# Half of the maximum's subtractions on VectorE in every block, and attention's context divided by its sums as it leaves PSUM

## The chip, the cores and the metric

The kernel runs on one core of one Trainium2 chip. A core has five engines that each work through a list of instructions of their own, in order: TensorE (PE, matrix products; its weight loads are listed apart as PEld), VectorE (DVE), ScalarE (ACT), GpSimd (POOL) and SyncE (SP), which here only issues DMA transfers. Engines wait for each other through semaphores. The metric is the time of one execution on the device in microseconds; the smaller, the better. The kernel before was run three times: 3268.8, 3256.43 and 3252.26 us, median 3256.43 us.

## The reference

One transformer layer in fp32: 2 sequences of 1024 tokens, width 1024, 32 heads of 32, and a gated feed-forward of 2752.

```
h   = layernorm(x)
qkv = h @ attn_qkvw + attn_qkvb                  # split into q, k, v, 32 heads of 32
scores = q @ k.T / sqrt(32)                      # per head, 1024 x 1024
probs  = softmax(scores)
x = x + (probs @ v) @ attn_ow + attn_ob
h = layernorm(x)
x = x + (silu(h @ W_gate.T) * (h @ W_up.T)) @ W_down.T
```

The softmax is the part that matters here: probs @ v = (exp(scores - max) @ v) / (sum of exp(scores - max)).

## The kernel before

**Blocks and units.** Tokens are worked on in four blocks of 512 (two sequences b, two halves blk). Attention of one block is 16 *units* (class Unit); a unit is two heads, 512 queries against 1024 keys, held as eight key tiles kt of 128 keys by 2 x 512 queries. A block then goes through the output projection and the feed-forward ("rest", lines 755 to 1148).

**A unit's way.** `scores` computes two key tiles at a time into PSUM; `largest` (L524, DVE) folds them into a running maximum `top`; `keep` (L529, ACT) copies them to SBUF as p. After the last tile `maximum` (L542 to L578) turns top, reduces it, and sends the negated maximum through DRAM to all partitions as `m`. Then, one key tile per beat, `less_maximum` (L580) adds m to p: L582 picks the engine, and `exponential` (L593, ACT) follows. `add` (L606) sums p over four neighbouring key tiles, on DVE for the last of each four (in the first block for all) and on POOL otherwise; the values are differenced to match (L599, POOL). `values` (L612) multiplies p by the values into the PSUM tile `acc`: columns 0 to 255 are the context, columns 256 to 511 the sums of p, by a matrix of ones, each sum repeated over the 32 rows of its head. There is one `acc` (bufs=1).

**From the accumulator to the projection.** `finish` (L638) copies acc to SBUF on ACT (L641) and later stores context and sums to DRAM (dctx L646, dsum L648). Every four units, `recip` (L703) loads the sums densely, takes reciprocals on DVE (L711) and stores them (drec). `load` (L719) brings a quarter of the context back with features on partitions (L722), loads each reciprocal row broadcast over 32 partitions (L726, eight loads a quarter), and POOL multiplies (L733). The event "prep" lets the output projection (`project` L782, products L785) start on that quarter.

**Order of the work.** Nothing is scheduled by hardware or compiler: the Emitter writes every engine's list in the order in which steps run here. Its clock counts only the planned cost of PE's steps (MM4 = 855 ns for a full product). `em.later(delay, fn)` issues fn when that clock has passed the delay. `run` takes side queues first (prep_ctx is one), then spreads the attention's beats (`paced`) evenly over the other work (`fill`). Attention of the first block runs beside the q, k and v projections; attention of blocks 2 to 4 runs beside the rest of blocks 1 to 3; the rest of block 4 runs alone. About 30 full products at the end of each rest (`late`, L1291) are held back and put ahead of the next projection.

**Feed-forward.** Gate and up are seven products of quarter matrices for each chunk of 128 features (Strassen-Winograd; `product`, L927), each ending in a PSUM tile that ACT (L939) or DVE (L941 to L954) reads out; silu is on ACT (L955), h = gate * up on DVE (L957). Every four chunks the down product follows in the same manner (`down7`, L1076): its PSUM tiles are added into x by DVE, one or two instructions each (L1089, L1091), and DVE forms four sums over h (L1045 to L1051). The last two chunks of a block use plain products (L1003, read out at L1014), and DVE puts x's halves right (L1032, L1034). All these products, the projections and the transposes (L259) share three PSUM tiles (`lps`, bufs=3).

Of the kernel before, what the change touches and what calls it, by code (L numbers as in the profile page):

```python
# [12 lines left out]
ALU = mybir.AluOpType  # L13
AX = mybir.AxisListType

P = 128
HEADS = 32
HD = 32
NH = 512
# [111 lines left out]
def preln_block_kernel(  # L131
# [14 lines left out]
    nc = tc.nc  # L146
# [64 lines left out]
    def dtile(shape, name):  # L211
        return dram.tile(shape, F32, tag=name, name=name)
# [4 lines left out]
    dv = {(b, hf): dtile([S, NH], f"dv{b}_{hf}") for b in range(B) for hf in range(NHF)}  # L217
    blocks = [(b, blk, i) for b in range(B) for blk in range(NS) for i in range(QTR)]
    dctx = {k: dtile([H // QTR, NH], "dctx%d_%d_%d" % k) for k in blocks}
    dsum = {k: dtile([HEADS // QTR, NH], "dsum%d_%d_%d" % k) for k in blocks}  # L220
    drec = {k: dtile([HEADS // QTR, NH], "drec%d_%d_%d" % k) for k in blocks}


    dws = [dtile([P, 4, NH], f"dws{c}") for c in range(NFULL)]
# [240 lines left out]
    class Unit:  # L465
# [113 lines left out]

        def less_maximum(self, kt):  # L580
            p = self.p[kt]
            eng = nc.vector if self.phase == 0 and kt % 4 == 3 else nc.gpsimd  # L582
            eng.tensor_tensor(p, p, self.m, ALU.add)  # L583
            em.later(3500.0, lambda: self.exponential(kt))
            if kt % SUMS > 0:

                vec = self.phase == 0 or kt % RUN == RUN - 1
                delay = 8100.0 if self.phase == 0 else 10000.0 if vec else 9500.0
                eng = nc.vector if vec else nc.gpsimd
                em.later(delay, lambda: self.add(kt, eng))  # L590
# [47 lines left out]
        def finish(self):  # L638
            part, n = divmod(self.u, UNITS // QTR)
            cs = Sm(f"cs_{self.name}")  # L640
            nc.scalar.copy(cs, self.acc)  # L641
            key = self.b, self.blk, part

            def store():
                ctx_ = dctx[key][n * 2 * HD : (n + 1) * 2 * HD, :]
                nc.sync.dma_start(ctx_.rearrange("f (a q) -> a f q", a=2), cs[:, :NQ])  # L646
                sums = dsum[key][2 * n : 2 * n + 2, :].rearrange("h (a q) -> a h q", a=2)
                nc.sync.dma_start(sums, cs[::HD, NQ:])  # L648

            em.later(2500.0, store, ("ctx", self.n))  # L650

# [48 lines left out]
    def prep_ctx(b):  # L700


        def recip(blk, i):  # L703
            cols = HEADS // QTR * NH // P
            sm = small([P, cols], "sums", 1, f"sums_{b}_{blk}_{i}")
            flat = lambda d: d.rearrange("h s -> (h s)").rearrange("(p c) -> p c", p=P)
            nc.sync.dma_start(sm, flat(dsum[b, blk, i]))
            rc = small([P, cols], "recs", 1, f"recs_{b}_{blk}_{i}")

            def go():  # L710
                nc.vector.reciprocal(rc, sm)  # L711
                nc.sync.dma_start(flat(drec[b, blk, i]), rc)

            em.later(11000.0, go, ("rec", b, blk, i))

        def alloc(blk):
            ctxT[b, blk] = T(f"ctx_{b}_{blk}")

        def load(blk, i):  # L719
            n = KC // QTR  # L720
            part = ctxT[b, blk][:, i * n : (i + 1) * n, :]
            nc.sync.dma_start(part, dctx[b, blk, i].rearrange("(g p) n -> p g n", p=P))  # L722
            recs = [Sm(f"rec_{b}_{blk}_{i}_{g}") for g in range(n)]
            for g, rec in enumerate(recs):
                for j in range(HPG):
                    nc.sync.dma_start(  # L726
                        rec[j * HD : (j + 1) * HD, :],
                        drec[b, blk, i][g * HPG + j, :].partition_broadcast(HD),
                    )

            def go():
                for g, rec in enumerate(recs):
                    nc.gpsimd.tensor_tensor(part[:, g, :], part[:, g, :], rec, ALU.mult)  # L733

            em.later(5000.0, go, ("mult", b, blk, i))
            em.later(8000.0, lambda: None, ("prep", b, blk, i))

        per = UNITS // QTR
        recips, loads = Steps(), Steps()
        for blk in range(NS):  # L740
            for i in range(QTR):
                n = (b * NS + blk) * UNITS + (i + 1) * per - 1
                recips.add(lambda blk=blk, i=i: recip(blk, i), needs=("ctx", n))
            if blk > 0:
                free = ("gu", b, blk - 1)
            else:
                free = ("half", B - 1) if b == 0 else ("gu", b - 1, NS - 1)
            loads.add(lambda blk=blk: alloc(blk), needs=free)
            for i in range(QTR):
                if i > 0:  # L750
                    loads.add(lambda: None, needs=("mult", b, blk, i - 1))
                loads.add(lambda blk=blk, i=i: load(blk, i), needs=("rec", b, blk, i))
        return recips, loads

    def oproj_steps(q, b, blk, st):
        st["w"] = {}
# [456 lines left out]
    with tc.manual_schedule():  # L1213

        head, fill, keep_qk = Steps(), Steps(), Steps()

        def two(fn, *args, **kw):

            q = Steps()
            fn(q, *args, **kw)  # L1220
            return q

        def ln_steps(q, b, t0, t1, tools, ahead):

            load, norm, turn, _ = tools
            for t in range(t0, t1):
                if t + ahead < t1:
                    q.add(lambda t=t + ahead: norm(t))
                turn(q, t)
                if t + 5 < NT:  # L1230
                    q.add(lambda t=t + 5: load(t))

        tools = load, norm, turn, _ = ln1(0)
        for t in range(4):
            head.add(lambda t=t: load(t))
        head.add(lambda: nc.sync.dma_start(bqk_t, b_qk))
        for _ in range(4):
            head.add(wst.next)
        head.add(lambda: load(4))
        for _ in range(8):  # L1240
            head.add(dst.next)
        for _ in range(5):
            head.add(wst.next)
        head.add(lambda: norm(0))
        ln_steps(head, 0, 0, TB, tools, 1)
        for _ in range(2):
            head.add(dst.next)
        qk_steps(head, 0, 0, [0])
        head.add(lambda: norm(TB))
        side = two(ln_steps, 0, TB, NT, tools, 1)  # L1250
        head.items += merged(two(v_steps, 0, 0, range(TB)), side).items
        qk_steps(head, 0, 0, [1])

        v_steps(fill, 0, 0, range(TB, NT))
        for g in range(1, G // 2):
            qk_steps(fill, 0, g)
        v_steps(fill, 0, 1)
        for g in range(G // 2, G - 2):
            qk_steps(fill, 0, g)

        tools = load1, norm1, turn1, stats1 = ln1(1)
        for t in range(5):
            fill.add(lambda t=t: load1(t))
        qk_steps(fill, 0, G - 2, [0])
        fill.items += merged(two(qk_steps, 0, G - 1, [0]), stats1(0, TB)).items
        last = two(qk_steps, 0, G - 2, [1])
        qk_steps(last, 0, G - 1, [1])
        fill.items += merged(last, two(ln_steps, 1, 0, TB, tools, 1)).items
        fill.items += merged(two(v_steps, 1, 0, range(2)), stats1(TB, TB)).items
        fill.items += merged(  # L1270
            two(v_steps, 1, 0, range(2, TB)), two(ln_steps, 1, TB, NT, tools, 1)
        ).items
        v_steps(fill, 1, 0, range(TB, NT))
        for g in range(0, G // 2):
            qk_steps(fill, 1, g)
        v_steps(fill, 1, 1)
        for g in range(G // 2, G - 2):
            qk_steps(fill, 1, g)
        for s in range(NS):
            for g in range(G - 2, G):  # L1280
                qk_steps(keep_qk, 1, g, [s])
            if s == 0:
                keep_qk.add(lambda: None, gives=("half", 1))

        def rest(n):

            q, late, st = Steps(), Steps(), {}
            b, blk = divmod(n, NS)
            turn = oproj_steps(q, b, blk, st)
            ffn_steps(q, b, blk, st, turn)  # L1290
            while late.cost < 30 * MM4:  # L1291
                late.items.insert(0, q.items.pop())
            return q, late


        rests = [rest(n) for n in range(B * NS)]
        lists = attention_steps([(n + 1) * UNITS * NT + 2 * NT for n in range(B * NS - 1)])
        side = [*prep_ctx(0), *prep_ctx(1)]
        em.run(head)
        em.run(fill, lists[0], side=(*side, weight_sum_steps()))  # L1300
        keep = keep_qk
        for (q, late), beats in zip(rests, [*lists[1:], None]):
            em.run(joined([keep, q]), beats, side=side)
            keep = late
        em.run(keep)
        em.settle(True)
# [51 lines left out]
```

## Time and profile before

| | |
|---|---|
| runs of the kernel, us | 3268.8, 3256.43, 3252.26 (median 3256.43) |
| profiled execution: span from first to last instruction, us | 3272.8 |
| its time beyond the span | not shown on the page; the span stands for the execution |
| mean granted TensorE clock | 0.986 |
| PE busy | 3166.3 us, 15488 products |
| DVE busy | 2012.2 us, 2733 instructions |
| ACT busy | 1446.8 us, 1585 instructions |
| POOL busy | 2039.6 us, 1079 instructions |
| subtraction of the maximum on POOL (L583) | 480 of 2508 ns |
| the same on DVE (first block only) | 32 of 1882 ns |
| copy of the accumulator on ACT (L641) | 64 of 588 ns |
| multiplication by the reciprocals on POOL (L733) | 32 of 1338 ns |
| DMA | 507.24 MB, mean 155 GB/s |

How to read it: the profile is one execution. A group's line gives source line, engine, operation, output<-input with shapes, count, then busy time and mean duration, then the idle time of the engine just before these instructions and what ended most of it. The 40 slices each stand for 3272.8 / 40 = 81.8 us; a digit is a busy share in tenths, and PEclk is the clock granted to TensorE in tenths of full speed. Stages by the timeline: first block's attention from 180 to 880 us, then boundary and rest of block 1 (880 to 1480), of block 2 (1480 to 2140), of block 3 (2140 to 2760), and of block 4 to the end. "Body" below means the stretches 1000 to 1480, 1640 to 2140 and 2310 to 2760 us.

### The profile page before, as it was taken

To read this page: it belongs to the slowest core of one execution; us is meant where nothing else is said; L and a number is where in the kernel's file an instruction comes from. 1 tells how busy PE (TensorE), PEld (TensorE's weight loads), DVE (VectorE), ACT (ScalarE), POOL (GpSimd) and SP (SyncE) were. 2 spreads that over 40 slices of the span, in tenths; PEclk is the share of its full clock that TensorE was granted. 3 is DMA by queue.
4 is the path that set the end of the run, shared out by engine and by line. 5 is a ranking of instruction groups with operands and counts; after the bars stand their busy time and mean duration, and the time that the engine had idled before them with its cause. 6 is when DMAs were issued, how large, how long until landed. Compare 5 with 4: busy or idle time off the path is not lost.

```text
span 3272.8 us, 42759 instructions
## 1 busy us (share of the span) xinstructions
PE 3166.3 (97%) x15488; PEld 1785.6 (55%) x15488; DVE 2012.2 (61%) x2733; ACT 1446.8 (44%) x1585; POOL 2039.6 (62%) x1079
## 2 busy tenths in 40 slices
PE   8999999999999999998899999988999999999999
PEld 4444434444346666563376655633756567477775
DVE  2266766776356777766577777666777774344334
ACT  2244554544456555563665555635655554010000
POOL 0267766777788777667887777777877777200000
PEclk9999999999999999998999999989999999999999
DMA  4566756655434554555344444562445445544452
GB/s 154 167 182 203 228 181 197 195 186 164 145 109 139 155 150 150 149 153 180 98 146 150 148 146 146 151 184 92 140 146 151 149 140 149 168 152 154 153 153 96
DMA packets 337825, 507.24 MB, mean 155 GB/s; under 512 B 105424, under 2 KB 122064, under 8 KB 337616
## 3 DMA queue, kind: packets, MB, share of 16 engines
q1 hardware_dynamic: 281424, 405.91, 40.4%
q10 hardware_dynamic: 56192, 98.60, 9.8%
q8 instruction: 124, 2.03, 0.3%
q14 instruction: 85, 0.70, 0.1%
HBM read 429.14 MB, written 75.24 MB: 154 GB/s over the span
## 4 chain that ended last, share of the span: by engine, by line
PE 79%; DVE 8%; POOL 4%; DMA 3%; issue 3%; ACT 2%; SPq 1%; ACTq 0%; POOLq 0%; DVEq 0%
PE p L927 30%; PE pq L371 13%; PE pd L1076 9%; PE acc L622 8%; PE s L510 7%; PE pvv L433 6%; PE po L785 4%; POOL p L583 2%; DVE x L1089 2%; DVE top L524 1%; DVE p L606 1%; PE pd L1003 1%; PE pg L971 1%; POOL p L606 1%; DVE h L957 1%
## 5 line engine op out<-in xcount | busy, mean ns | idle before, releaser
L583 POOL TENSOR_TENSOR p<-p,m 128x1024 f32<-128x1024 f32 x480 | 1197.0, 2508 | 15.9 <-DMA m<-d 15.9
L529 ACT COPY p<-s 128x1024 f32<-128x1024 f32 x512 | 516.3, 1012 | 730.0 <-DVE top L524 553.6
L593 ACT ACTIVATE p<-p 128x1024 f32<-128x1024 f32 x512 | 529.6, 1056 | 379.2 <-POOL p L583 325.6
L606 POOL TENSOR_TENSOR p<-p,p 128x1024 f32<-128x1024 f32 x192 | 466.8, 2431 | 352.5 <-ACT p L593 346.8
L524 DVE TENSOR_TENSOR top<-s,top 128x1024 f32<-128x1024 f32 x384 | 469.1, 1222 | 289.0 <-PE s L510 272.0
L927 PE MATMUL p<-sum,m 128*128 128x256 f32 x2688 | 610.4, 382 | 1.4 <-ACT gate L939 0.9
L927 PEld LDWEIGHTS p<-sum,m 128*128 128x128 f32 x2688 | 505.2, 190 | 101.1 <-issue 29.3
L927 PE MATMUL p<-xn2T,m 128*128 128x256 f32 x2016 | 469.5, 384 | 0.3 <-ACT xn2T L267 0.2
L371 PE MATMUL pq<-xnT,wqk 128*128 128x512 f32 x1024 | 457.4, 599 | 0.0
L1076 PE MATMUL pd<-wp,h 128*128 128x512 f32 x960 | 432.6, 598 | 15.2 <-DVE x L1089 15.0
L927 PEld LDWEIGHTS p<-xn2T,m 128*128 128x128 f32 x2016 | 382.6, 192 | 87.0 <-issue 29.8
L606 DVE TENSOR_TENSOR p<-p,p 128x1024 f32<-128x1024 f32 x192 | 328.1, 1709 | 105.2 <-ACT p L593 70.4
L371 PEld LDWEIGHTS pq<-xnT,wqk 128*128 128x128 f32 x1024 | 190.2, 190 | 249.4 <-issue 247.7
L510 PE MATMUL s<-q,k 32*128 32x512 f32 x2048 | 312.6, 650 | 12.0 <-ACT p L529 12.0
L1076 PEld LDWEIGHTS pd<-wp,h 128*128 128x128 f32 x960 | 177.7, 190 | 251.1 <-issue 197.0
L1189 POOL TENSOR_TENSOR ws<-raw 128x512 f32<-128x512 f32 x62 | 89.8, 1448 | 298.3 <-DMA raw<-in_w_gu 190.7
L1089 DVE TENSOR_TENSOR x<-pd,x 128x512 f32<-128x512 f32 x360 | 235.7, 680 | 52.6 <-PE pd L1076 52.2
L622 PE MATMUL acc<-p,vals 128*32 128x256 f32 x4096 | 254.6, 389 | 11.3 <-DVE p L606 11.3
L433 PE MATMUL pvv<-wv,xnT 128*128 128x512 f32 x512 | 231.1, 601 | 0.2 <-DVE vv L445 0.2
L785 PE MATMUL po<-wo,ctx 128*128 128x512 f32 x512 | 229.7, 601 | 0.8 <-DMA wo<-in_w_o 0.8
L622 PEld LDWEIGHTS acc<-p,vals 128*32 128x32 f32 x4096 | 121.4, 111 | 181.6 <-issue 97.7
L990 POOL MEMSET h<- 64x512 f32 x4 | 2.1, 524 | 298.9 <-PE pd L1076 298.9
(94 smaller groups left out, 2520.2 us busy)
## 6 DMA issues: line engine op xcount, KB each, us to landing
m<-dws SPq DMA_DIRECT2D x336, 256.0 KB
m<-in_w_gu SPq DMA_DIRECT2D x252, 256.0 KB
wp<-ddn SPq DMA_DIRECT2D x160, 256.0 KB
m<-d SPq DMA_DIRECT2D x64, 512.0 KB
wp<-in_w_dn SPq DMA_DIRECT2D x120, 256.0 KB
raw<-in_w_gu ACTq DMA_DIRECT2D x84, 256.0 KB
dws<-ws ACTq DMA_DIRECT2D x84, 256.0 KB
x<-in_x SPq DMA_DIRECT2D x32, 512.0 KB
```

Source lines behind the costliest of these rows:

```text
L371: nc.tensor.matmul(ps, wqk[b, g, w, hk][:, k, :], xnT[b, s][:, kc, :], start=(kc == 0), stop=(kc == KC - 1),)
L433: nc.tensor.matmul(st["ps"], xnT[b, t // TB][:, kc, (t % TB) * P : (t % TB + 1) * P], st["w"][kc], start=(kc == 0), stop=(kc == KC - 1),)
L510: nc.tensor.matmul(ps[a][:, h * NH : (h + 1) * NH], self.k[rows, i * P : (i + 1) * P], self.q[rows, :], start=True, stop=True,)
L524: nc.vector.tensor_tensor(self.top, s, self.p[0] if kt == 1 else self.top, ALU.max)
L529: nc.scalar.copy(self.p[kt], s)
L583: eng.tensor_tensor(p, p, self.m, ALU.add)
L593: nc.scalar.activation(self.p[kt], self.p[kt], AF.Exp, scale=SCALE)
L606: eng.tensor_tensor(self.p[kt], self.p[kt], self.p[kt - 1], ALU.add)
L622: nc.tensor.matmul(self.acc[j * HD : (j + 1) * HD, c : c + NQ], w(h), self.p[kt][:, q0 : q0 + NQ], start=start, stop=stop, skip_group_chec ...
L785: nc.tensor.matmul(st["ps"], ctxT[b, blk][:, g, t * P : (t + 1) * P], st["w"][hf, g], start=(g == 0), stop=(g == G - 1),)
L927: nc.tensor.matmul(ps, mats[c, n][:, kc, :], rhs, start=(kc == 0), stop=(kc == hk - 1),)
L1076: nc.tensor.matmul(st["pd"], lefts[n](pi)[:, j, t * P : (t + 1) * P], st["wp", pi, n, j], start=(j == 0), stop=(j == PART // 2 - 1),)
```

## The change

Two things change. In `less_maximum`, DVE took key tiles 3 and 7 in the first block and none after it; now it also takes the odd key tiles (1, 3, 5, 7) of the units of blocks 2 to 4. In `finish`, the context is divided by its sums as it leaves PSUM: DVE takes the reciprocal of the 256 columns of sums and multiplies the 256 columns of context by it. The copy on ACT, the sums' way through DRAM, the broadcast loads, and POOL's multiplication fall away. The quarter's context is loaded as soon as its store has been issued; no quarter waits for the multiplication of the one before; "prep" comes 6000 ns of planned time after the load instead of 8000.

```diff
         def less_maximum(self, kt):
             p = self.p[kt]
-            eng = nc.vector if self.phase == 0 and kt % 4 == 3 else nc.gpsimd
+            mine = kt % 4 == 3 if self.phase == 0 else kt % 2 == 1
+            eng = nc.vector if mine else nc.gpsimd
             eng.tensor_tensor(p, p, self.m, ALU.add)
...
             cs = Sm(f"cs_{self.name}")
-            nc.scalar.copy(cs, self.acc)
+            nc.vector.reciprocal(cs[:, NQ:], self.acc[:, NQ:])
+            nc.vector.tensor_tensor(cs[:, :NQ], self.acc[:, :NQ], cs[:, NQ:], ALU.mult)
...
                 nc.sync.dma_start(ctx_.rearrange("f (a q) -> a f q", a=2), cs[:, :NQ])
-                sums = dsum[key][2 * n : 2 * n + 2, :].rearrange("h (a q) -> a h q", a=2)
-                nc.sync.dma_start(sums, cs[::HD, NQ:])
...
-        def recip(blk, i):
...
-            def go():
-                nc.vector.reciprocal(rc, sm)
-                nc.sync.dma_start(flat(drec[b, blk, i]), rc)
-
-            em.later(11000.0, go, ("rec", b, blk, i))
...
             nc.sync.dma_start(part, dctx[b, blk, i].rearrange("(g p) n -> p g n", p=P))
-            recs = [Sm(f"rec_{b}_{blk}_{i}_{g}") for g in range(n)]
...
-            def go():
-                for g, rec in enumerate(recs):
-                    nc.gpsimd.tensor_tensor(part[:, g, :], part[:, g, :], rec, ALU.mult)
-
-            em.later(5000.0, go, ("mult", b, blk, i))
-            em.later(8000.0, lambda: None, ("prep", b, blk, i))
+            em.later(6000.0, lambda: None, ("prep", b, blk, i))
...
-                if i > 0:
-                    loads.add(lambda: None, needs=("mult", b, blk, i - 1))
-                loads.add(lambda blk=blk, i=i: load(blk, i), needs=("rec", b, blk, i))
-        return recips, loads
+                n = (b * NS + blk) * UNITS + (i + 1) * per - 1
+                loads.add(lambda blk=blk, i=i: load(blk, i), needs=("ctx", n))
+        return loads
```

More of the change, by code (lines that the diff above doesn't have):

```diff
@@ L219, in preln_block_kernel @@
     dctx = {k: dtile([H // QTR, NH], "dctx%d_%d_%d" % k) for k in blocks}
-    dsum = {k: dtile([HEADS // QTR, NH], "dsum%d_%d_%d" % k) for k in blocks}
-    drec = {k: dtile([HEADS // QTR, NH], "drec%d_%d_%d" % k) for k in blocks}
     dws = [dtile([P, 4, NH], f"dws{c}") for c in range(NFULL)]
@@ L700, in prep_ctx @@
     def prep_ctx(b):
-        def recip(blk, i):
[L704 to L708, printed above, removed]
-            def go():
-                nc.vector.reciprocal(rc, sm)
-                nc.sync.dma_start(flat(drec[b, blk, i]), rc)
-            em.later(11000.0, go, ("rec", b, blk, i))
         def alloc(blk):
@@ L722, in load @@
             nc.sync.dma_start(part, dctx[b, blk, i].rearrange("(g p) n -> p g n", p=P))
-            recs = [Sm(f"rec_{b}_{blk}_{i}_{g}") for g in range(n)]
-            for g, rec in enumerate(recs):
[L725 to L729, printed above, removed]
-            def go():
-                for g, rec in enumerate(recs):
-                    nc.gpsimd.tensor_tensor(part[:, g, :], part[:, g, :], rec, ALU.mult)
-            em.later(5000.0, go, ("mult", b, blk, i))
-            em.later(8000.0, lambda: None, ("prep", b, blk, i))
+            em.later(6000.0, lambda: None, ("prep", b, blk, i))
         per = UNITS // QTR
-        recips, loads = Steps(), Steps()
+        loads = Steps()
         for blk in range(NS):
-            for i in range(QTR):
-                n = (b * NS + blk) * UNITS + (i + 1) * per - 1
-                recips.add(lambda blk=blk, i=i: recip(blk, i), needs=("ctx", n))
             if blk > 0:
@@ L1297, in preln_block_kernel @@
         lists = attention_steps([(n + 1) * UNITS * NT + 2 * NT for n in range(B * NS - 1)])
-        side = [*prep_ctx(0), *prep_ctx(1)]
+        side = [prep_ctx(0), prep_ctx(1)]
         em.run(head)
```

## The prediction

> **What bounds the kernel now.** I read the page from the top: busy shares, the 40 slices, the chain that ended last. Then the waits of the whole span, the stages with a low PE digit, and the stretches in which the kernel multiplies by the down weights.
>
> ```profile
> span 3272.8 us, 42759 instructions
> ...
> PE 3166.3 (97%) x15488; PEld 1785.6 (55%) x15488; DVE 2012.2 (61%) x2733; ACT 1446.8 (44%) x1585; POOL 2039.6 (62%) x1079
> ...
> PE   8999999999999999998899999988999999999999
> ...
> PEclk9999999999999999998999999989999999999999
> ...
> PE 79%; DVE 8%; POOL 4%; DMA 3%; issue 3%; ACT 2%; SPq 1%; ACTq 0%; POOLq 0%; DVEq 0%
> ```
>
> TensorE (PE) is the bound: 97% busy, 79% of the chain. The change touches no matmul, so it can only move the 3272.8 - 3166.3 = 106.5 us in which PE is idle, and the granted clock behind those gaps. DVE at 61% and POOL at 62% look free, but that is a mean over stages. Both low digits of PE and of the clock lie where one 512-token block ends and the next begins. The view by windows, cut at the stages, says how low (columns: window, PE, PEld, DVE, ACT, POOL, clock, DMA share, GB/s):
>
> ```profile
> 1480.00:1640.00 160.00, 135.43 (x631) 59.20 (x628) 96.60 (x124) 74.37 (x80) 127.66 (x70) 0.91 0.43 134
> 1640.00:2140.00 500.00, 491.90 (x2840) 311.71 (x2839) 362.48 (x516) 282.63 (x301) 389.68 (x195) 1.00 0.50 149
> 2140.00:2310.00 170.00, 141.49 (x662) 64.86 (x661) 103.33 (x123) 79.66 (x87) 128.21 (x70) 0.90 0.41 128
> ```
>
> At the boundaries POOL is at 75 to 80%, PE idles 25 and 29 us, and the clock is 0.91 and 0.90, which costs about 0.09 x 160 = 14 and 0.10 x 170 = 17 us more. The timeline of the second boundary shows why (start, duration, engine, line; in brackets the idle time before and its releaser):
>
> ```profile
> 2164.30 1.26 POOL L733 TENSOR_TENSOR ctx<-ctx,rec 128x512 f32<-128x512 f32 x1 [5.52 <-DMA rec<-drec]
> ...
> 2175.72 3.35 DVE L606 TENSOR_TENSOR p<-p,p 128x1024 f32<-128x1024 f32 x1 [11.50 <-POOL p L606]
> ...
> 2179.73 2.07 PE L1003 MATMUL pd<-wd,h 128*128 128x512 f32 x2 [11.70 <-DVE x L1014]
> ```
>
> POOL stands at L733 for the broadcast reciprocals, its subtractions behind that are late, DVE stands in L606 for POOL's sum, DVE's evacuation (L1014) is queued behind, and PE waits 11.70 us for it. The same row costs 8.48 us at 1516.
>
> **What goes.** (1) The detour of the sums: 64 stores, 16 loads and 16 stores of them, 128 broadcast loads on SP's queue, 16 reciprocals (5.5 us of DVE), 32 multiplications on POOL (42.5 us) with 97.2 us of waiting for DMA. What stops PE through it, by PE's gaps in the timeline: 3.2 + 8.5 at 1500 to 1516, 1.7 + 11.7 at 2156 to 2168, and 8.4 at 2243 where POOL, still late, ran ops back to back and one DVE addition took 12.18 us: 33.5 us. The trace's records of the granted clock have half-clock stretches at these gaps (6.8, 10.2, 13.7, 3.4, 10.2 us) cost half of 44.3 = 22 us. At 885 to 900, where POOL also waits for rec, 3.2 us of gaps and half a 6.8 us window are 6.6 us. That is 62 us at most. What is late next there are DVE's own evacuations in the last down stretch and the last token tile's layernorm (pt_f waits for ACT gate L939, 15.3 us in all, untouched). I take 45 us, and 20 as the lower bound. Before the new loads, prep needs 6 us of planned time instead of 8, and PE holds over 25 us of held-back matmuls (30 x 0.855) to cover them; uncovered, each of the 4 blocks could lose one landing, a few us.
>
> (2) POOL gives up 4 of 8 subtractions in 48 units: 192 x 2.5 = 480 us, off the path in the body, where PE is 98 to 99% busy. It is worth something at the boundaries alone, within the 45.
>
> (3) ACT's 64 copies cs<-acc at 0.588 us: 38 us off ACT (44% busy), worth nothing by themselves.
>
> **What comes, all on DVE.** (a) 192 subtractions. The row for them is L583 DVE in the first block: x32, mean 1882 ns beside a POOL busy 72%; at best they take what L606 takes when POOL is quiet, 1216 ns. In the body POOL falls to about half busy, so I take 1.7. (b) 64 times a reciprocal of 128x256 and a product of 128x256 from PSUM. The product has a row, L949: 424 ns. The reciprocal has 128x32 at 342 ns and 128x4 at 178: (342 - 178) / 28 = 5.9 ns a column, so 178 + 252 x 5.9 = 1.65 us; bounds are 0.42 (any other 128x256) and 8 x 0.342 = 2.74. Together 2.07 us.
>
> The Trainium skill (VectorE: DVE Perf Modes, on the fixed hardware budget) says that reciprocal repeats its divide 8 times; at the 0.96 GHz of its page Trainium Kernel Development and Optimization (NeuronCore Architecture), 256 columns would be an estimated 2.13 us instead of 1.65, some 31 us more over 64 units. The skill also speaks against (a): by its page SBUF — State Buffer (two separate sides), a DVE op with two SBUF inputs and a POOL op exclude each other for the whole instruction, so the moved work would still wait for POOL. The rows agree as far as they go: h (L957) takes 0.69 us at the end without POOL and 1.24 to 1.69 beside it.
>
> Is there room? A unit (two heads) takes some 39.7 us in the body, DVE is busy 72% there, about 28.4 us. 4 x 1.7 + 2.07 = 8.9 us more, less some 0.7 us of shorter waits for POOL, makes 36.6, 92%. That fits on average, but not where it counts. The stretches of down products (L1076) have two DVE evacuations for many PSUM tiles and four sums over h. The windows view of the 14 such stretches that run beside attention (the last rows and their sum):
>
> ```profile
> 2376.80:2409.50 32.70, 31.09 (x122) 12.27 (x121) 31.60 (x40) 13.80 (x16) 22.91 (x10) 1.00 0.42 130
> 2475.80:2506.60 30.80, 30.71 (x122) 12.46 (x121) 29.89 (x40) 15.61 (x17) 23.00 (x13) 1.00 0.53 157
> 2572.80:2604.90 32.10, 31.03 (x122) 12.44 (x121) 30.95 (x40) 14.20 (x16) 22.54 (x9) 1.00 0.44 135
> 2672.30:2703.30 31.00, 30.64 (x122) 12.55 (x121) 29.17 (x41) 15.81 (x16) 25.97 (x14) 1.00 0.44 137
> sum 458.80, PE 440.70 PEld 179.70 DVE 418.09 ACT 205.88 POOL 321.18; mean PE 31.48 PEld 12.84 DVE 29.86 ACT 14.71 POOL 22.94
> ```
>
> DVE is busy 418.1 of 458.8 us, 91%; 40.7 us are free, and PE already loses 18.1 us waiting for evacuations. 96 maxima (L524) start in these stretches, 96 / 7 = 13.7 units. They bring 55 subtractions (67 us at 1.22, 104 at 1.89) and 13.7 x 2.07 = 28 us. POOL goes from 70% to (321 - 55 x 2.36) / 459 = 42%; of about 45 us by which the sums over h exceed their 0.68 us, some 18 go. Net 77 to 114 us, middle 95. Of the 40.7 free us a third to all can be used, since DVE runs in order and some idle time lies before the products end; and DVE may come out of each stretch 1 us later than now (the three PSUM buffers are already used up: lags of 4 to 6 us). So PE loses 95 - 41 - 14 = 40 to 95 - 12 - 14 = 69 us more, and I take 55; with the ends of both prices 22 to 88. In the product stretches (L927) DVE is busy 4 to 8 us of 10 and most of 2 to 5 us more fits: 8 us, 0 to 15.
>
> Queued behind each reciprocal, which waits for the accumulator, are the subtraction and the next evacuations; scores and both maxima are issued ahead of it and outlast the accumulator's 2.5 us, so the wait is about nothing. The store of cs comes 1.5 us later or more and holds SP's queue, with weights loaded several tiles ahead as cover. In the first block only 2.07 us a unit are added, on a DVE busy 459 of 700 us: 0, up to 5. DVE's first subtraction follows POOL's by one beat; POOL waited only 15.9 us for m in all, but DVE is less late than POOL: 0 to 10, I take 0.
>
> **Sum.** -45 + 55 + 8 + 0 = +18 us against the profiled execution: 3272.8 becomes 3291. The page gives only its span, no time around it, and that is 16 us above the median; as a difference on the median: 3256.4 + 18 = 3274.
>
> **Rivals.**
> - *Down stretches hold DVE's load (faster).* It decides if the subtractions cost about 1.22 us (POOL half idle, few waits) and all free time is used: loss 77 - 41 - 14 = 22, gain 55 to 62. Net about -36: 3220. For it: POOL's own lateness makes many of DVE's waits. Against: 91% busy already, and PE idle there. It turns below 45 us of loss. 0.30.
> - *DVE bound through the whole body.* Each subtraction waits for a POOL op, or for m at the boundaries, and the product stretches cannot drain the lag: loss 88 + 15 + 5, gain 30: +78, 3334. For it: 92% and about 0.9 us of unavoidable waiting for silu per chunk. 0.17.
> - *Nothing arrives.* The stalls at the boundaries are re-made by the next late engine and DVE's work finds room: 3256. 0.08.
> - Forecast, slower by a little: 0.45, its own range 3258 to 3300.
>
> About 0.5% (16 us) is what a measurement of this kernel can tell from no change. Of the forecast's 0.45, 0.27 lies over that and 0.18 within; of the first rival 0.28 is faster, 0.02 within. Faster 0.28, same 0.28, slower 0.44. The range takes in the first two rivals' middles: 3222 to 3335.
>
> **What would show it.** Right: L733 and L711 gone, no gap over 5 us at the boundaries and clock above 0.95 there; L583 DVE at 1.5 to 1.9 us x224; a reciprocal of about 1.65 us; DVE over 95% and PE's idle time 60 to 90 us in the 14 stretches. Wrong: PE idle below 45 us there (first rival), or PE below 97% between the stretches too (second). A reciprocal far from 1.65 us, or a boundary that still idles 25 us, would each refute a term.

## The result and the profile after

The changed kernel takes 3312.77 us (median of 4 runs, 3310.75 to 3314.07) against 3256.74 us before (4 runs): ratio 1.0154, 95% interval 1.0131 to 1.0178, 56 us slower. The sign was forecast; the size was not (18 us). From the page of the changed kernel, the lines that answer to those shown of before:

```profile
span 3310.0 us, 42267 instructions
...
PE 3173.4 (96%) x15488; PEld 1775.4 (54%) x15488; DVE 2339.7 (71%) x3037; ACT 1416.2 (43%) x1521; POOL 1601.0 (48%) x855
...
PE   8999989999999999998899999988999999999999
...
PEclk9999999999999999999999999999999999999999
...
PE 73%; DVE 21%; ACT 3%; issue 2%; DMA 1%; ACTq 0%; SPq 0%; DVEq 0%
```

PE still sets the end, but DVE's part of the chain went from 8 to 21%. The digits of the clock no longer dip. The same two boundaries in the view by windows, here cut from the end of a block's last full down stretch to the next block's first gate product (window, PE, PEld, DVE, ACT, POOL, clock, DMA share, GB/s), first before, then after:

```profile
1497.70:1618.90 121.20, 105.21 (x464) 43.20 (x464) 70.03 (x88) 60.46 (x64) 105.42 (x56) 0.93 0.42 133
2153.80:2284.30 130.50, 107.20 (x466) 43.41 (x465) 77.31 (x87) 59.10 (x63) 103.06 (x56) 0.90 0.39 121
```

```profile
1513.80:1620.60 106.80, 101.20 (x466) 41.43 (x464) 85.14 (x99) 51.87 (x54) 71.15 (x36) 0.97 0.39 125
2186.90:2295.40 108.50, 101.55 (x465) 41.62 (x463) 87.51 (x104) 51.82 (x54) 71.33 (x36) 0.97 0.39 124
```

The boundaries are 14 and 22 us shorter with the same products, PE's idle time there falls from 16 and 23 to 6 and 7 us, and POOL's busy time from 105 and 103 to 71 us. So what was meant to be won was won. The loss is inside the blocks. The 15 stretches of gate and up products of blocks 1 to 3, last line of the same view for before, then after:

```profile
sum 1080.90, PE 1064.24 PEld 781.62 DVE 673.76 ACT 651.03 POOL 859.62; mean PE 70.95 PEld 52.11 DVE 44.92 ACT 43.40 POOL 57.31
```

```profile
sum 1124.80, PE 1073.33 PEld 776.11 DVE 855.73 ACT 641.72 POOL 632.30; mean PE 71.56 PEld 51.74 DVE 57.05 ACT 42.78 POOL 42.15
```

And the 14 down stretches, after (before: 458.8 us, PE 440.7, DVE 418.1, shown with the prediction):

```profile
sum 503.10, PE 453.96 PEld 178.84 DVE 479.25 ACT 209.21 POOL 229.54; mean PE 32.43 PEld 12.77 DVE 34.23 ACT 14.94 POOL 16.40
```

Product stretches +44 us, down stretches +44 us, everything else 1733 to 1682 us, -51: together the 37 us by which the profiled spans differ. Of the first 44 us, 35 are idle time of PE (17 us before, 51 after) and 9 are longer busy time; of the second, 31 (18 before, 49 after) and 13. Part of the 13 is the clock: it is 1.00 in all 14 down stretches before, and 0.91 to 0.96 in four of them after, which by their rows is worth some 8.5 us (an estimate). The second stretch, before and after:

```profile
1164.70:1196.90 32.20, 30.49 (x122) 12.52 (x121) 30.35 (x39) 14.52 (x16) 22.57 (x10) 1.00 0.46 138
1165.80:1204.10 38.30, 33.28 (x122) 13.19 (x121) 35.62 (x46) 14.21 (x15) 16.11 (x8) 0.91 0.35 108
```

In the down stretches DVE is 95% busy; in the product stretches it is 76% busy on average and PE idles 51 us all the same. PE waits for the reading-out (evacuation) of its PSUM tiles. In the view of waits (us in total, times, longest us), first the down products, before and after, then two of the gate and up products after, where before has nothing over 0.9 us (L1044, L1057 and L895 are before's L1076, L1089 and L927):

```profile
PE pd L1076 <- DVE x L1089: 17.9, 26, 1.7
PE pd L1044 <- DVE x L1057: 47.5, 43, 5.0
...
PE p L895 <- DVE gate L918: 6.8, 6, 2.3
PE p L895 <- DVE gate L911: 4.9, 5, 1.7
```

What that looks like in a product stretch: the timeline of DVE in the changed kernel, at the end of a unit.

```profile
1865.17 2.56 DVE L522 TENSOR_TENSOR top<-s,top 128x1024 f32<-128x1024 f32 x2 [0.57 <-PE s L508]
1867.64 1.75 DVE L640 RECIPROCAL cs<-acc 128x256 f32<-128x256 f32 x1
1869.42 0.42 DVE L641 TENSOR_TENSOR cs<-acc,cs 128x256 f32<-128x256 f32 x1
1869.76 3.03 DVE L582 TENSOR_TENSOR p<-p,m 128x1024 f32<-128x1024 f32 x1
1872.71 0.41 DVE L911 TENSOR_TENSOR gate<-p,gate 128x256 f32<-128x256 f32 x1
```

Two maxima, the reciprocal, the product and the subtraction of key tile 3 stand in one beat, 7.6 us in which no feed-forward tile is read out (L911 is the first again). PE meanwhile works 2.3 us on the accumulator and fills its three PSUM tiles (24 matmuls), then waits:

```profile
1867.36 5.45 PE L895 MATMUL p<-sum,m 128*128 128x256 f32 x24
1873.18 1.13 PE L895 MATMUL p<-sum,m 128*128 128x256 f32 x4 [0.37 <-DVE gate L911]
```

In this unit the beat just fits, and PE waits 0.37 us; in the unit at 1656, with the same five instructions, it waits 1.53 us. Counted over the trace, 31 such beats lie in product stretches, and 17 us of PE's idle time there stand directly behind them (within ten DVE instructions from the reciprocal on). Another 12 us stand further on, while DVE is still late or waits; 22 us (15 before) stand ahead of the transposes behind layernorm.

The subtraction is 3.03 us long in the unit shown. By key tile, the mean over 48 units is 1.40 us for tile 1, 2.26 for 3, 1.23 for 5 and 1.94 for 7: 45 of the 48 subtractions of tile 3 start while POOL is inside an instruction.

### The profile page after: what moved, and what is told of

It is laid out like the page before. It is cut to its first block, busy times and chain, and to the rows that moved or that the text cites. A ratio compares the mean times of both kernels' runs of the same rounds, so it can differ in the third digit from the quotient of the medians.

```text
span 3310.0 us, 42267 instructions
## 1 busy us (share of the span) xinstructions
PE 3173.4 (96%) x15488; PEld 1775.4 (54%) x15488; DVE 2339.7 (71%) x3037; ACT 1416.2 (43%) x1521; POOL 1601.0 (48%) x855
## 4 chain that ended last, share of the span: by engine, by line
PE 73%; DVE 21%; ACT 3%; issue 2%; DMA 1%; ACTq 0%; SPq 0%; DVEq 0%
PE p L895 25%; PE pq L369 12%; PE pd L1044 8%; PE s L508 7%; PE pvv L431 6%; PE po L753 6%; PE acc L621 6%; DVE top L522 4%; DVE p L582 4%; DVE x L1057 3%; DVE cs L640 2%; PE pd L971 1%; DVE p L605 1%; ACT p L527 1%; DVE part L548 1%
## 5 line engine op out<-in xcount | busy, mean ns | idle before, releaser
L605 POOL TENSOR_TENSOR p<-p,p 128x1024 f32<-128x1024 f32 x192 | 494.7, 2576 | 849.9 <-ACT p L592 837.2
L582 POOL TENSOR_TENSOR p<-p,m 128x1024 f32<-128x1024 f32 x288 | 746.4, 2597 | 20.9 <-DMA m<-d 17.3
L895 PE MATMUL p<-sum,m 128*128 128x256 f32 x2688 | 616.1, 383 | 18.0 <-ACT gate L907 5.2
L895 PEld LDWEIGHTS p<-sum,m 128*128 128x128 f32 x2688 | 502.7, 190 | 126.4 <-issue 29.7
L895 PE MATMUL p<-xn2T,m 128*128 128x256 f32 x2016 | 468.9, 383 | 13.8 <-DVE gate L918 4.5
L1044 PE MATMUL pd<-wp,h 128*128 128x512 f32 x960 | 442.3, 606 | 40.6 <-DVE x L1057 39.0
L895 PEld LDWEIGHTS p<-xn2T,m 128*128 128x128 f32 x2016 | 378.2, 190 | 106.0 <-issue 27.9
L582 DVE TENSOR_TENSOR p<-p,m 128x1024 f32<-128x1024 f32 x224 | 385.7, 1722 | 0.0
L605 DVE TENSOR_TENSOR p<-p,p 128x1024 f32<-128x1024 f32 x192 | 290.4, 1512 | 73.8 <-ACT p L592 68.9
L1044 PEld LDWEIGHTS pd<-wp,h 128*128 128x128 f32 x960 | 177.5, 191 | 286.1 <-issue 189.8
L1057 DVE TENSOR_TENSOR x<-pd,x 128x512 f32<-128x512 f32 x360 | 234.5, 679 | 40.1 <-PE pd L1044 40.0
L621 PE MATMUL acc<-p,vals 128*32 128x256 f32 x4096 | 254.3, 390 | 0.0
L621 PEld LDWEIGHTS acc<-p,vals 128*32 128x32 f32 x4096 | 121.9, 111 | 168.2 <-issue 93.1
```

The lines of the kernel that those rows point to most:

```text
L605: eng.tensor_tensor(self.p[kt], self.p[kt], self.p[kt - 1], ALU.add)
L621: nc.tensor.matmul(self.acc[j * HD : (j + 1) * HD, c : c + NQ], w(h), self.p[kt][:, q0 : q0 + NQ], start=start, stop=stop, skip_group_chec ...
L895: nc.tensor.matmul(ps, mats[c, n][:, kc, :], rhs, start=(kc == 0), stop=(kc == hk - 1),)
L1044: nc.tensor.matmul(st["pd"], lefts[n](pi)[:, j, t * P : (t + 1) * P], st["wp", pi, n, j], start=(j == 0), stop=(j == PART // 2 - 1),)
```

## The experiments

Two theories at first. **Burst**: the place matters, too much of DVE's work stands in the beat of the division. **Load**: each microsecond given to DVE costs alike. The table has the time, its ratio to before with the interval, and from each profile the 15 product stretches, the 14 down stretches and the rest of the span, in us. Each ratio is to runs of the kernel before that were taken beside it (medians 3256.7 to 3263.6 us), so a difference of two medians below carries a few us.

| kernel | median | ratio (95%) | product | down | rest |
|---|---|---|---|---|---|
| before (profiled run) | 3256.74 | 1 | 1080.9 | 458.7 | 1733.2 |
| before_2 | 3259.98 | one run | 1079.5 | 458.1 | 1720.5 |
| before_3 | 3269.1 | one run | 1080.2 | 457.8 | 1729.3 |
| changed | 3312.77 | 1.0154 (1.0131-1.0178) | 1124.8 | 503.1 | 1682.1 |
| div_only | 3250.11 | 0.9971 (0.9954-0.9987) | 1084.7 | 484.3 | 1676.9 |
| sub_only | 3275.86 | 1.0047 (1.0033-1.0061) | 1088.5 | 487.9 | 1697.8 |
| no_kt3 | 3261.13 | 1.0000 (0.9987-1.0013) | 1089.6 | 491.7 | 1679.8 |
| no_kt5 | 3320.04 | 1.0180 (1.0163-1.0198) | 1121.2 | 507.8 | 1683.8 |
| sub3_later | 3289.98 | 1.0084 (1.0063-1.0105) | 1113.4 | 493.3 | 1682.0 |
| even | 3312.91 | 1.0155 (1.0131-1.0179) | 1108.4 | 514.1 | 1687.5 |
| late_div | 3287.53 | 1.0078 (1.0054-1.0102) | 1110.3 | 495.8 | 1671.8 |
| late_only | 3234.13 | 0.9908 (0.9886-0.9930) | 1078.2 | 467.1 | 1687.1 |
| late_no_kt3 | 3268.48 | 1.0028 (1.0018-1.0038) | 1107.8 | 484.0 | 1681.3 |
| late_kt5 | 3236.18 | 0.9929 (0.9914-0.9945) | 1081.6 | 476.3 | 1677.0 |
| no_pool_adds | 3256.60 | 0.9987 (0.9975-0.9999) | 1096.4 | 478.0 | 1680.9 |
| late_dummy | 3282.77 | 1.0075 (1.0055-1.0095) | 1088.7 | 506.4 | 1684.8 |
| adds_later | 3355.99 | 1.0279 (1.0248-1.0310) | 1138.7 | 524.2 | 1692.1 |
| late_only_19 | 3248.82 | 0.9963 (0.9943-0.9983) | 1080.6 | 473.0 | 1685.2 |

**One part alone, and one key tile less.**

```diff
# div_only (on the changed kernel)      # no_kt3: kt in (1, 5, 7); no_kt5: kt in (1, 3, 7)
-            mine = kt % 4 == 3 if self.phase == 0 else kt % 2 == 1
+            mine = self.phase == 0 and kt % 4 == 3
# sub_only (on the kernel before)
-            eng = nc.vector if self.phase == 0 and kt % 4 == 3 else nc.gpsimd
+            mine = kt % 4 == 3 if self.phase == 0 else kt % 2 == 1
+            eng = nc.vector if mine else nc.gpsimd
```

> The division at the accumulator alone; the subtractions stay on POOL as before, but for key tiles 3 and 7 of the first block. The changed kernel lost 44 us in the product stretches and 45 us in the down stretches and won 51 us at the boundaries, profile against profile. Theory 'burst': in one beat of each unit DVE has two maxima, the reciprocal (1.75 us), the product (0.42 us) and a subtraction of up to 3.3 us, together more than the three PSUM tiles cover; PE stalls there. Without the subtraction this beat fits: 10 us lost in the product stretches, 10 in the down stretches, the boundary gain of 35 to 50 us stays, so 15 to 30 us faster than before. Theory 'load': every microsecond given to DVE costs alike; this part is 104 of 434 us in the blocks with feed-forward, so 24% of 89 us, 21 us lost, boundary gain kept: also about 15 to 30 us faster. Theory 'POOL': the boundaries were won by POOL's fewer subtractions, not by the detour's end; then this one is no faster than before.

> The subtractions of the odd key tiles on DVE alone; context divided by its sums as before, by way of DRAM, broadcast loads and POOL. 'Load': 330 of 434 us, 76% of 89 us, 68 us lost, and little won at the boundaries because POOL still waits for the broadcast loads: 45 to 70 us slower. 'Burst': without reciprocal and product in that beat most of the 44 us in the product stretches is gone, the down stretches keep some 35 us: 20 to 45 us slower. 'POOL': the boundary gain of 40 us or more is here, so within 20 us of before.

> The changed kernel, but key tile 3 goes back to POOL in the blocks with feed-forward (DVE subtracts 1, 5 and 7). Key tile 3 is the one whose subtraction shares a beat with reciprocal and product. 48 subtractions, 83 us, less on DVE. 'Load': a fifth of the loss comes back, 15 to 20 us faster than the changed kernel, the same as without key tile 5. 'Burst': most of the product stretches' 44 us comes back, 30 to 45 us faster than the changed kernel, and 20 us or more faster than the one without key tile 5.

> The changed kernel, but key tile 5 goes back to POOL in the blocks with feed-forward (DVE subtracts 1, 3 and 7): as much work off DVE as without key tile 3, but from a beat without reciprocal. 'Load': 15 to 20 us faster than the changed kernel, as without key tile 3. 'Burst': 0 to 12 us faster than the changed kernel.

The division alone is faster by 0.3%, less than both theories said, for it loses 26 us in the down stretches; but its rest falls to 1677, so the end of the detour wins the boundaries by itself, and "POOL", which denied that, falls. The subtractions alone cost 0.5%, 16 us: under what "load" and "burst" said, and within the 20 us of "POOL", for their rest falls too, to 1698, 23 to 35 us under before's. So relief of POOL alone wins much of the same stalls. The parts would add up to 1.0018; together they are 1.0154, some 44 us more than their sum. Key tile 3 decides: without it the kernel is 52 us faster than the changed one, without tile 5 it is 7 us slower, with the same number of instructions off DVE (neither theory had the second slower). First the last line of the view of the product stretches in no_kt3, then no_kt5's subtractions on DVE in the view of groups (count, then busy us and mean ns):

```profile
sum 1089.60, PE 1065.21 PEld 781.02 DVE 816.15 ACT 640.31 POOL 681.44; mean PE 71.01 PEld 52.07 DVE 54.41 ACT 42.69 POOL 45.43
```

```profile
L582 DVE TENSOR_TENSOR p<-p,m 128x1024 f32<-128x1024 f32 x176 | 331.0, 1881 | 0.0
```

no_kt3's 1089.6 us are within 9 us of before. no_kt5's subtractions take 1881 ns each, no_kt3's 1644. "Load" in its simple form is refuted. But two things make tile 3 what it is: its beat and its waiting for POOL.

**The same work in another place.**

```diff
# sub3_later, on the changed kernel: kt 3 in later blocks, its exponential as much later
-            eng.tensor_tensor(p, p, self.m, ALU.add)
+            em.later(2500.0, lambda: eng.tensor_tensor(p, p, self.m, ALU.add))
# even: kt % 2 == 0 instead of kt % 2 == 1
# late_div, on the changed kernel (late_only: with div_only's choice of engine)
-            nc.vector.reciprocal(cs[:, NQ:], self.acc[:, NQ:])
-            nc.vector.tensor_tensor(cs[:, :NQ], self.acc[:, :NQ], cs[:, NQ:], ALU.mult)
+            nc.scalar.copy(cs, self.acc)
+            em.later(14000.0, divide)      # the same two, on cs in SBUF
...
-            em.later(2500.0, store, ("ctx", self.n))
+            em.later(14000.0 + 2500.0, store, ("ctx", self.n))
```

> The changed kernel with one thing moved and nothing taken out: in the blocks with feed-forward the subtraction of key tile 3, still on DVE, is issued 2.5 us of planned time later, past the next evacuations, and its exponential as much later. DVE's work is the same to the instruction. 'Burst': the product stretches' loss of 44 us falls below 20, 25 to 45 us faster than the changed kernel. 'Load' (the sum of DVE's work, or the waiting of this one subtraction for POOL wherever it stands): within 10 us of the changed kernel.

> The changed kernel with the even key tiles (0, 2, 4, 6) on DVE in the blocks with feed-forward instead of the odd ones: as many subtractions, but in the beats without scores, maxima and reciprocal. 'Burst': product stretches lose under 20 us instead of 44, 25 to 45 us faster than the changed kernel, unless key tile 0 waits for the maximum to land. 'Load': within 10 us of the changed kernel.

> The changed kernel with the division moved instead of the subtraction: ACT copies the accumulator as before, and DVE's reciprocal and product work on the copy in SBUF 14 us of planned time (three beats) later, the store after them. 'Burst': the product stretches lose under 15 us, 35 to 50 us faster than the changed kernel. 'Load': within 10 us of the changed kernel, or slower by what the product of two SBUF operands waits for POOL.

> Late division as above, all subtractions of the blocks with feed-forward on POOL. Against the division at the accumulator alone (0.9971 of before, with 23 us lost in the down stretches) 'burst' expects some of those 23 us back, since reciprocal and maxima no longer share a beat: 5 to 15 us faster than it, 0.992 to 0.996 of before. 'Load': the same as it, 0.997.

Moving the subtraction, or the division, out of the shared beat gives 23 and 25 us back, not the 25 to 50 of "burst", and the product stretches keep 29 to 33 of their 44 us instead of falling below 20. Even key tiles give nothing: the product stretches lose 16 us less, the down stretches 11 more. In sub3_later the subtraction of tile 3 also gets shorter, 1.84 instead of 2.26 us, so it does not part place from waiting; in late_div it keeps its 2.34 us, so there the gain is one of place. What late_div still loses in the product stretches is 20 us of idle and 9 us of longer busy time of PE. 14 us of the idle time stand behind a new shared beat, for the moved division mostly meets key tile 7's subtraction and again two maxima (DVE, then PE's wait):

```profile
2324.79 1.74 DVE L644 RECIPROCAL cs<-cs 128x256 f32<-128x256 f32 x1
2326.57 2.28 DVE L645 TENSOR_TENSOR cs<-cs 128x256 f32<-128x256 f32 x1
2328.77 0.41 DVE L916 TENSOR_TENSOR gate<-p,gate 128x256 f32<-128x256 f32 x1
2329.10 2.54 DVE L522 TENSOR_TENSOR top<-s,top 128x1024 f32<-128x1024 f32 x2
2331.55 1.81 DVE L582 TENSOR_TENSOR p<-p,m 128x1024 f32<-128x1024 f32 x1
...
2333.76 2.77 PE L900 MATMUL p<-xn2T,m 128*128 128x256 f32 x6 [2.48 <-DVE up L920]
```

So place is worth tens of us, but less than "burst" said, since the other beats are not free. late_only is the version that beats both kernels, 0.9908, a little more than "burst" said: its division stands where late_div's does, but no subtraction meets it, its product stretches are as before and its down stretches lose 8 us. From its page:

```profile
span 3232.4 us, 42400 instructions
...
PE 3147.9 (97%) x15488; PEld 1776.6 (55%) x15488; DVE 2176.6 (67%) x2845; ACT 1444.7 (45%) x1585; POOL 1997.9 (62%) x1047
```

DVE does more there than in div_only (2176.6 against 2109.5 us, mostly since its product now reads two SBUF operands and takes 1.24 us instead of 0.42), and the kernel is 16 us faster. That ACT's copy frees the accumulator sooner does not explain it: in neither trace does PE wait for the accumulator to be read.

**Waiting for POOL, or bare length?**

```diff
# late_no_kt3: late_div with kt in (1, 5, 7); late_kt5: late_div with kt == 5
# no_pool_adds, on the changed kernel: POOL's additions left out, so the output is not the reference's
-            eng.tensor_tensor(self.p[kt], self.p[kt], self.p[kt - 1], ALU.add)
+            if self.phase == 0 or kt % RUN == RUN - 1:
+                eng.tensor_tensor(self.p[kt], self.p[kt], self.p[kt - 1], ALU.add)
# late_dummy, on late_only, behind the subtraction on POOL
+            if self.phase > 0 and kt % 2 == 1:
+                nc.vector.tensor_reduce(
+                    idle, self.m.rearrange("p (b j) -> p b j", j=HD), AX.X, ALU.max
+                )
```

> Late division, and DVE subtracts key tiles 1, 5 and 7 in the blocks with feed-forward: late_div without key tile 3. So far key tile 3's subtraction takes 2.3 us on DVE wherever the division stands, key tile 5's 1.25. 'Own price': key tile 3 costs by itself, through its waits for POOL, so taking it away helps here too: 35 to 50 us faster than late_div, about 3240 to 3252. 'Shared beat': it costs only beside the division, which is no longer there: 8 to 20 us faster than late_div, about 3268 to 3280.

> Late division, and of the blocks with feed-forward only key tile 5 on DVE, the one that hardly waited for POOL. 'Waits': it fits, within 8 us of late_only (3234), perhaps a little faster since POOL has less to do. 'Load': a quarter of the 53 us between late_only and late_div, 10 to 16 us slower than late_only.

> The changed kernel with POOL's additions of neighbouring key tiles left out in the blocks with feed-forward (key tiles 1, 2, 5 and 6 are not summed, so the output there is not the reference's); DVE's list is unchanged to the instruction. It prices DVE's waiting for POOL. 'Waits': DVE's subtractions fall from 1.72 to about 1.3 us and the kernel gains 25 to 45 us on the changed one. 'Load' (the bare length of DVE's instructions): DVE still has the same list, 0 to 12 us.

> late_only with one more DVE instruction where the odd key tiles' subtractions stood: a maximum over m in groups of 32, 128x1024, about 1.35 us, whose result nobody reads; one SBUF operand, a kind that did not wait for POOL so far. All subtractions stay on POOL. 'Load': most of the 53 us by which late_div is slower than late_only comes with it: 3265 to 3290. 'Waits': 3234 to 3252.

late_no_kt3 is 19 us faster than late_div, as "shared beat" said, and in the product stretches only 2.5 us, where it was 35 beside the division (no_kt3). Of the 27 us that remain there, 14 are, as in late_div, idle time of PE behind the beat of the division and tile 7. late_kt5 costs 2 us on late_only, as "waits" said, but that is a sum: its stretches lose 13 us and its rest is 10 us shorter, and the subtraction took 1.49 us. no_pool_adds gives back all 56 us, more than "waits" said; tile 3's subtraction falls from 2.26 to 1.26 us (44 of 48 start with POOL idle), though the mean of all only to 1.58 and not to the 1.3 expected, and the product stretches lose 15 instead of 44 us, with DVE's list unchanged. Since POOL's part of the whole work falls as well, the 56 us are an upper bound for the waits. late_dummy shows the other half (groups of late_dummy, mean ns second after the bar):

```profile
L585 DVE TENSOR_REDUCE idle<-m 128x32 f32<-128x1024 f32 x192 | 231.5, 1205 | 0.0
```

192 instructions of 1.2 us that never wait for POOL cost 49 us on late_only, nearly as much as the subtractions in late_div (53), as "load" said and against "waits". But they cost it elsewhere: down stretches 506.4 instead of 467.1, product stretches only 1088.7 instead of 1078.2, though DVE is busy 865.7 us there, more than the 855.7 of the changed kernel. So each theory has its stage: in the down stretches bare length is enough to lose as much (waits add to it, no_pool_adds is 25 us shorter there), and in the product stretches it is not: there place and waits count.

**What was still open.**

```diff
# adds_later, on the changed kernel
-                delay = 8100.0 if self.phase == 0 else 10000.0 if vec else 9500.0
+                delay = 8100.0 if self.phase == 0 else 13000.0 if vec else 12500.0
# late_only_19: 19000.0 instead of 14000.0; before_2, before_3: the kernel before
```

> The kernel before once more, for a second profile. The profiled execution of before lasted 16 us longer than its median, and the differences of spans (37 us for the changed kernel, against 56 us of the medians) carry that. If the boundaries vary from execution to execution, a span near 3256 has boundaries that are some 15 us shorter and the same down and product stretches, and the gain at the boundaries is nearer 35 than 51 us.

> The same again, a third profile: boundaries (from the last down stretch of a block to the next block's first product) vary by 10 us or more between the profiles, everything else by less than 5 us.

> The changed kernel with every addition of neighbouring key tiles issued 3 us of planned time later in the blocks with feed-forward; nothing left out, DVE's and POOL's work the same. In the changed kernel 45 of 48 subtractions of key tile 3 find POOL inside an instruction. 'Waits in the shared beat': with POOL's additions moved out of that beat the subtraction of key tile 3 falls from 2.26 to below 1.7 us, the product stretches lose under 30 us instead of 44, 15 to 40 us faster than the changed kernel. 'Load': within 10 us of it. If the subtraction does not get shorter, this says nothing.

> late_only with the division 19 instead of 14 us of planned time after the accumulator, one beat on, in a beat with scores and maxima. 'Shared beat': a few us slower than late_only, 3236 to 3245. 'Load': the same, 3232 to 3236.

before_2 spans 3258.1 us: its product and down stretches are within 2 us of the first profile, its rest is 13 us shorter; before_3 lies between (rest 1729.3). The boundaries of before vary by that much from execution to execution, and the profile on which the prediction rests is one of the long ones. Against before_2 the rest fell by 38 us, the stretches grew by 90, together the 52 us between the spans and nearly the 56 of the medians. adds_later is the slowest of all at 1.0279; tile 3's subtraction only fell to 2.12 us, so it doesn't part waiting from place, but the same additions, issued later, cost 43 us more; PE also waits 16 us for them at the accumulator (L621). late_only_19 is 15 us slower than late_only by the medians, in the direction of "shared beat" and more than it said; but its 10 runs spread from 3240.6 to 3263.7 us, and its profiled one, the fastest, is only 6 us longer than late_only's.

## Why the prediction was wrong in size

- **Boundary gain: right, somewhat high.** 45 forecast; 51 against the profiled execution, 38 against one near the median. The detour's stalls are gone, and what was named as next (the transposes behind layernorm, pt_f, which wait for ACT gate) stayed, with gaps of 7.2 and 6.1 us against "no gap over 5 us". I set the sum of a long execution on the median.
- **Down stretches: right.** 55 forecast, range 22 to 88; measured +44. But PE's idle time there is 49 us where I named 60 to 90 as the sign: it grew by 31 us, and 13 us are longer busy time, partly the clock, which the sum did not have. DVE is 89 to 97% busy.
- **Prices: right.** Subtraction 1.72 us (1.7 taken), reciprocal 1.747 us (1.65 taken), product 0.424 us. The reciprocal waited 5.5 us in all for the accumulator, "about nothing" as said. The Trainium skill's repeat of 8 (VectorE: DVE Perf Modes, on the fixed hardware budget) gave an estimated 2.13 us; the runs show 1.747, and the measurement decides.
- **The step that failed:** "In the product stretches (L927) DVE is busy 4 to 8 us of 10 and most of 2 to 5 us more fits: 8 us, 0 to 15." Measured: 44. The sum went by means over 10 us and by a mean subtraction. I had worked out, correctly, that both maxima are issued ahead of the reciprocal, but only to show that it doesn't wait; that this makes 7.6 us without a read-out, in a pipeline with three PSUM tiles, I did not add up. And 1.7 us is a mean over key tiles from 1.23 to 2.26, the longest in just that beat. The trace puts 17 of the 44 us directly behind the beat, 12 of idle time further on, 7 more ahead of layernorm's transposes, and 9 in PE's longer busy time; without the division or without tile 3 all but 8 or 9 us of it goes. The four kernels that part it, by their product stretches above before: division without tile 3 (no_kt3) 9 us, tile 3 without division (sub_only) 8, both with a short tile 3 (no_pool_adds) 15, both with a long one 44.
- **The sign: partly luck.** With the measured boundaries and down stretches the forecast's own 8 us would have made -51 + 44 + 8 = +1 us (against before_2: -38 + 45 + 8 = +15). That the kernel is clearly slower comes from the term that failed.
- **The rivals.** "DVE bound through the whole body" (3334) was nearest: it named subtractions that each wait for a POOL op and product stretches that can't drain the lag. Its sign, PE below 97% between the stretches, is there: 1073.3 of 1124.8 us is 95.4%. But DVE is not bound there, at 76%. "Down stretches hold" fails by its total and, narrowly, by its sign (49 us of idle time where it set 45); "nothing arrives" is refuted.
- **Open.** No run shortens tile 3's waits and changes nothing else, so how the loss beside the division divides between its bare 1.2 us and its waits is bounded by no_pool_adds alone. Why PE's busy time in the product stretches grows by 9 us was not settled either.

## What to carry to other kernels

Price added work by the beat in which it is issued, not by the engine's mean share: lay out what stands on that engine between two read-outs of PSUM and compare it with what the PSUM tiles cover. Place can be worth as much as load: the same division makes the kernel 0.3% faster right behind the accumulator and 0.9% faster three beats later, and two edits that win 0.3% and lose 0.5% alone lose 1.5% together. Before setting a sum of one profile on a median, see whether that profile is a typical execution.

## What the runs showed of the hardware

- An fp32 reciprocal of 128x256 takes 1.745 to 1.758 us from PSUM and 1.74 from SBUF, a product of PSUM and SBUF 0.42, the same product of two SBUF operands 1.24 on average beside a busy POOL.
- In the changed kernel the 98 subtractions (two SBUF operands) that DVE began while POOL was idle took 1.20 to 1.22 us, the 126 others 1.20 to 3.37; in adds_later one took 5.50 us, across two operations of POOL, so more than one of them can go ahead of a waiting subtraction. The maximum with one SBUF operand (late_dummy) took 1.20 to 1.22 us all 192 times. The Trainium skill (SBUF — State Buffer, two separate sides) says that the one that starts first holds the shared pair of ports for its whole instruction; these durations agree.
